# Linear attention in a decoder block: the division by the sums, with features on partitions instead of tokens

## The chip, the cores and the metric

The kernel runs on one core of a Trainium2 chip. The metric is the device time of one execution in microseconds (us). A core has five engines that run side by side and meet only at semaphores: TensorE (PE in the profile; its weight loads are PEld), VectorE (DVE), ScalarE (ACT), GpSimd (POOL) and SyncE (SP), which here only issues DMAs. Each engine works through its own instructions strictly in the order in which the program gives them, so an instruction that waits also holds up everything behind it on its engine.

## The reference

A decoder layer over 32 batches of 128 tokens with 256 features, in float32: a causal linear attention (part A), a cross attention with softmax (part B), and a gated feed-forward network, each behind a layer normalization and with a residual.

```python
def attn(x, Wq, bq, Wk, bk, Wv, bv, Wo, bo):       # 16 heads of 16 features
    q, k, v = heads(x @ Wq.T + bq), heads(x @ Wk.T + bk), heads(x @ Wv.T + bv)
    q, k = elu(q) + 1, elu(k) + 1
    kv_cum = cumsum(k[..., :, None] * v[..., None, :], axis=2)
    k_cum = cumsum(k, axis=2)
    num = einsum('bhsd,bhsde->bhse', q, kv_cum)
    den = einsum('bhsd,bhsd->bhs', q, k_cum)
    return merge(num / (den[..., None] + 1e-6)) @ Wo.T + bo

x = x + attn(layernorm(x), ...)
x = x + xattn(layernorm(x), ctx, ctx, ...)          # softmax(q k^T / 4) v, 16 heads
x = x + ffn(layernorm(x), ...)                      # w1, w2, h1, h2, w3 with row scales
```

What the change touches is the last line but one of `attn`: the division of `num` by `den` and the product with `Wo`.

## The kernel before

The work has two stages. Up to about 440 us the two attentions of all 32 batches are computed, two batches (a *pair*, index m or n) at a time; after that the feed-forward network runs over eight blocks of four batches. The residual stream x of all batches stays in SBUF (`xs`).

**Part A, linear attention, for one pair.** `a_norm` takes the statistics on DVE (`pair_stats`; the inverse root by Newton steps on POOL) and normalizes on POOL. `a_transpose` puts features on partitions. `a_keys` and `a_queries` project (`project`) and apply `phi`: two ScalarE passes and one DVE pass; the queries are then masked on POOL by head parity (`masked`, factors in `col`). `a_values` projects with tokens on partitions into `va`, where each head has 32 columns: 16 values, then 16 ones. For each batch j of the pair:

- `a_scores(m, j)`: products of keys and queries into four PSUM banks (`scores_banks`, tag s0 and s1, one buffer of each), in the profile *sa*. DVE multiplies by the causal mask into `at` (L494).
- `a_weighted(m, j)` calls `weighted`: 16 small products (*pf*, L404) with `at` as the moving operand. The result has features on partitions: in each group g of 32 partitions 16 rows of a head's numerator and 16 rows that all hold its denominator (from the ones). ScalarE copies it to SBUF as `fa` (L412).
- `a_divide(m, j)` calls `divided`: four PE transposes (*po*, L419) put tokens on partitions; DVE adds epsilon (L423), inverts the 16 denominators of each token (L424) and multiplies (L428) into `oa`.
- `a_turn(m, j)`: two transposes (*pot*, L512) put features on partitions again; ScalarE copies to `oT` (L514).
- `a_out(m, j)`: the product with Wo (*pw*, L367 from L518), which DVE adds to x (L519).

**Part B, cross attention**, has the same shape with a softmax: `b_maxima` computes the scores once (*sm*) and reduces their maxima on DVE (L565); `b_turn_maxima` transposes these (*pz*) and spreads them into `mT` (L576); `b_scores` computes the scores again minus the maxima (*se*, L388 and L588) and ScalarE takes the exponent (L598); `b_weighted` and `b_divide` are as in part A, with `fb` and `ob`. *sm*, *sa* and *se* share the same four PSUM banks, so each has to wait until the one before has been read. All other PSUM tiles come from four buffers (`bank`).

**What sets the order.** `manual_schedule` makes the order in the program the order of PE, ACT, DVE and POOL. It is written out by hand as lists of units, each (function, pairs ahead, batch). The list `both` is one step of the steady state (L613): part A works on pair m, part B on pair m-3, and each step has two halves, one for each batch. `first` (L621) is for the first three steps, `begins` (L646), `alone` and `last` for those in which the feed-forward network already starts. A unit that has been done is skipped. SP's DMAs are not in such a list; they are issued in an order that the compiler chooses, each when its buffers are free. On SP's queue there are the loads of x, weights and context (`cT`, b_load), the second loads of weights, which DVE compares with the first (`again`, `test`), and the stores of the output.

```python
both = [
    (b_maxima, 0, 0), (b_weighted, -1, 1), (a_divide, -1, 1), (b_transpose, 1), (b_values, 1),
    (a_scores, 0, 0), (b_turn_maxima, 0, 0), (b_divide, -1, 1), (a_turn, -1, 1), (a_transpose, 1),
    (b_queries, 1), (b_scores, 0, 0), (a_weighted, 0, 0), (a_out, -1, 1), (b_norm, 2), (a_keys, 1),
    (b_maxima, 0, 1), (b_weighted, 0, 0), (a_divide, 0, 0), (a_bias, 1), (a_queries, 1),
    (a_scores, 0, 1), (b_turn_maxima, 0, 1), (b_divide, 0, 0), (a_turn, 0, 0), (b_keys, 1),
    (b_scores, 0, 1), (a_weighted, 0, 1), (a_out, 0, 0), (a_norm, 2), (a_values, 1), (b_load, 2),
]
```

The functions that the change touches, and what calls them:

Of the kernel before, what the change touches and what calls it, by code (L numbers as in the profile page):

```python
# [32 lines left out]
A_TAGS = {"xna", "xTa", "e", "r", "ka", "qa2", "at0", "at1", "fa", "oa", "oT"}  # L33
# [13 lines left out]
def decoder_block_kernel(  # L47
# [30 lines left out]
    warms = tiny.tile([P, 2], F32, name="warms")  # L78
    zero, warm = warms[:, 0:1], warms[:, 1:2]
# [182 lines left out]
    with tc.manual_schedule(engines=ORDERED):  # L262
# [133 lines left out]
        def weighted(weights, v, tag):  # L396

            pf = bank("pf")
            for i in range(4):
                for g in range(G):
                    nc.tensor.matmul(  # L404
                        pf[32 * g : 32 * g + 32, i, :],
                        lhsT=v[:, 4 * i + g, :],
                        rhs=weights[g // 2][:, g % 2, i, :],
                        start=True,
                        stop=True,
                    )  # L410
            f = buffer([P, 4, S], F32, tag=tag, name=tag)
            nc.scalar.copy(f, pf)  # L412
            return f

        def divided(f, add, tag):

            po = bank("po")
            for i in range(4):
                nc.tensor.transpose(po[:, i, :], f[:, i, :], ident)  # L419
            po = po.rearrange("p i (g w) -> p (i g) w", w=VW)  # L420
            rden = small.tile([P, H], F32, tag="rden", name="rden", bufs=2)
            if add:
                nc.vector.tensor_scalar(rden, po[:, :, HD], add, None, ALU.add)  # L423
                nc.vector.reciprocal(rden, rden)  # L424
            else:
                nc.vector.reciprocal(rden, po[:, :, HD])
# [75 lines left out]
        def a_weighted(m, j):  # L502
            A[m]["f", j] = weighted(A[m].pop(("w", j)), A[m]["v"][:, j], "fa")

        def a_divide(m, j):
            A[m]["o", j] = divided(A[m].pop(("f", j)), ATTN_EPS, "oa")

        def a_turn(m, j):
            pt = bank("pot").rearrange("p a s -> p (a s)")[:, : DC * S]
            o = A[m].pop(("o", j))  # L510
            for c in range(DC):
                nc.tensor.transpose(pt[:, ts(c, P)], o[:, ts(c, P)], ident)  # L512
            oT = buffer([P, DC, S], F32, tag="oT", name="oT")
            nc.scalar.copy(oT.rearrange("p c s -> p (c s)"), pt)  # L514
            A[m]["oT", j] = oT

        def a_out(m, j):
            pp = token_major(bank("pw").rearrange("p a s -> p (a s)")[:, :D], WO, A[m].pop(("oT", j)))  # L518
            nc.vector.tensor_tensor(xs[m][:, j, :], pp, xs[m][:, j, :], ALU.add)  # L519
# [52 lines left out]
        def b_turn_maxima(m, j):  # L572
            pz = bank("pz").rearrange("p a s -> p (a s)")[:, :S]
            nc.tensor.transpose(pz, zs[j].rearrange("p g r -> p (g r)"), ident)
            mT = buffer([P, 4, S], F32R, tag="mT", name="mT")
# [28 lines left out]
        def b_divide(m, j):  # L604
            o = divided(Bs[m].pop(("f", j)), None, "ob")
# [8 lines left out]
            (b_maxima, 0, 0), (b_weighted, -1, 1), (a_divide, -1, 1), (b_transpose, 1), (b_values, 1),  # L614
            (a_scores, 0, 0), (b_turn_maxima, 0, 0), (b_divide, -1, 1), (a_turn, -1, 1), (a_transpose, 1),
            (b_queries, 1), (b_scores, 0, 0), (a_weighted, 0, 0), (a_out, -1, 1), (b_norm, 2), (a_keys, 1),
            (b_maxima, 0, 1), (b_weighted, 0, 0), (a_divide, 0, 0), (a_bias, 1), (a_queries, 1),
            (a_scores, 0, 1), (b_turn_maxima, 0, 1), (b_divide, 0, 0), (a_turn, 0, 0), (b_keys, 1),
            (b_scores, 0, 1), (a_weighted, 0, 1), (a_out, 0, 0), (a_norm, 2), (a_values, 1), (b_load, 2),
        ]  # L620
        first = [  # L621
            (a_scores, 0, 0), (a_norm, 2), (a_turn, -1, 1), (a_keys, 1), (a_out, -1, 1), (b_norm, 2),
            (a_weighted, 0, 0), (a_bias, 0), (a_scores, 0, 1), (a_divide, 0, 0), (a_queries, 1),
            (b_transpose, 1), (a_values, 1), (a_weighted, 0, 1), (a_turn, 0, 0), (a_bias, 1),
            (b_queries, 1), (a_transpose, 2), (a_out, 0, 0), (a_divide, 0, 1), (b_load, 2),
# [12 lines left out]
        def settle():  # L638
# [303 lines left out]
```

## Time and profile before

| | us |
|---|---|
| median of the runs | 1135.98 (1135.59 to 1137.45, 3 runs) |
| the profiled execution, as timed | 1138.04 |
| span of its profile | 1136.2 |
| granted TensorE clock, mean | 0.997 of full speed |
| L428 DVE product oa<-po,rden, 128x256 | 0.425 each, 32 times |
| L412 ACT copy fa<-pf, 128x512 | 0.592 each, 32 times |
| L514 ACT copy oT<-pot, 128x256 | 0.373 each, 32 times |
| L519 DVE x<-pw,x, 128x256 | 0.425 each, 32 times |
| L565 DVE reduction nm<-sm, 128x1024 | 1.217 each, 64 times |

A line of the groups reads: line of the kernel, engine, operation, output<-inputs, shapes and count, then busy time in all and the mean of one in ns, then the idle time of that engine just before these instructions and what ended it. A line of the order in time reads: start, length, engine, line, operation, names, shapes and count, and in brackets the idle time before it with its releaser. Matmuls are pipelined: a group of four transposes of 0.27 us each takes 0.66 us, and the next group starts before that time is over, so what a group costs is read from the distance between the starts of successive groups. A line of busy time by stretches gives the stretch and its length, then busy time and count of PE, PEld, DVE, ACT and POOL, then the granted TensorE clock, the share of the DMA engines and GB/s.

### The profile page before, as it was taken

The numbers are of one execution on the slowest core, as the hardware profiler recorded it, in microseconds if no ns is written. First come the engines' busy times: TensorE is split into PE (matmuls) and PEld (weight loads), VectorE is DVE, ScalarE is ACT, GpSimd is POOL, SyncE is SP. The second block draws the span as 40 slices with busy tenths as digits, with TensorE's granted clock in tenths as the row PEclk, the third lists the DMA queues.
The fourth block names the chain that finished last, engine by engine and source line by source line (L and its number), as shares of the span: only waits on it lengthen the run. The fifth ranks groups of instructions, "written<-read, shape, count | busy, mean of one in ns | idle before, by whom it ended". The sixth has DMA issues, their size and how long they took to land.

```text
span 1136.2 us, 20345 instructions
## 1 busy us (share of the span) xinstructions
PE 1117.1 (98%) x8238; PEld 902.7 (79%) x8238; DVE 577.3 (51%) x1296; ACT 411.4 (36%) x655; POOL 446.8 (39%) x1025
## 2 busy tenths in 40 slices
PE   8899999999999999999999999999999999999997
PEld 6677777777777777767888888888888888888886
DVE  6667777777777776532243433522522522422411
ACT  4344444444444446861221221321311312312311
POOL 3655555555555546454231321321311312312311
PEclk9999999999999999999999999999999999999999
DMA  8001111111111100005000111000000000000000
GB/s 274 1 20 48 47 48 48 48 48 48 48 48 48 48 11 11 1 1 185 20 26 31 38 38 38 19 14 5 29 5 5 19 1 2 18 1 15 5 1 22
DMA packets 26548, 39.28 MB, mean 35 GB/s; under 512 B 2512, under 2 KB 18640, under 8 KB 26448
## 3 DMA queue, kind: packets, MB, share of 16 engines
q1 hardware_dynamic: 22000, 26.09, 6.8%
q0 software_dynamic: 4032, 11.54, 3.2%
q8 instruction: 67, 1.10, 0.4%
q10 hardware_dynamic: 416, 0.28, 0.1%
q14 instruction: 33, 0.27, 0.1%
HBM read 33.71 MB, written 4.19 MB: 33 GB/s over the span
## 4 chain that ended last, share of the span: by engine, by line
PE 88%; DVE 3%; POOL 3%; ACT 2%; issue 2%; DMA 1%; SPq 0%; POOLq 0%; DVEq 0%; ACTq 0%
PE ph L218 47%; PE pp L359 9%; PE py L762 5%; PE pf L404 5%; PE pv L367 4%; PE se L388 3%; PE sa L388 3%; PE sm L388 3%; PE pw L367 3%; PE po L419 2%; PE pt L349 1%; DMA H<-in_h2T_dram 1%; DVE at L494 1%; PE se L588 1%; DVE nm L565 1%
## 5 line engine op out<-in xcount | busy, mean ns | idle before, releaser
L181 DVE TENSOR_TENSOR gl<-hg,gh 128x512 fp32r<-128x512 f32 x126 | 87.7, 696 | 345.5 <-POOL gh L180 342.6
L180 POOL CAST gh<-hg 128x512 fp32r<-128x512 f32 x128 | 79.1, 618 | 362.0 <-ACT hg L242 362.0
L242 ACT ACTIVATE hg<-ph,col 128x512 f32<-128x512 f32 x128 | 88.3, 690 | 366.8 <-PE ph L218 366.8
L218 PE MATMUL ph<-sl,H 128*128 128x512 f32 x512 | 199.3, 389 | 0.8 <-POOL sl L181 0.8
L218 PE MATMUL ph<-gl,H 128*128 128x512 f32 x512 | 199.4, 389 | 0.4 <-DVE gl L181 0.4
L218 PE MATMUL ph<-sh,H 128*128 128x512 f32 x512 | 199.6, 390 | 0.1
L218 PE MATMUL ph<-gh,H 128*128 128x512 f32 x512 | 199.4, 390 | 0.0
L218 PEld LDWEIGHTS ph<-sl,H 128*128 128x128 f32 x512 | 96.1, 188 | 21.0 <-POOL sl L181 1.2
L218 PEld LDWEIGHTS ph<-gl,H 128*128 128x128 f32 x512 | 96.1, 188 | 21.0 <-DVE gl L181 1.1
L218 PEld LDWEIGHTS ph<-sh,H 128*128 128x128 f32 x512 | 96.1, 188 | 20.9 <-POOL sh L180 0.6
L218 PEld LDWEIGHTS ph<-gh,H 128*128 128x128 f32 x512 | 96.1, 188 | 20.4 <-POOL gh L180 0.6
L218 PE MATMUL ph<-xh,W 128*128 128x512 f32 x256 | 100.6, 393 | 0.0
L218 PE MATMUL ph<-xl,W 128*128 128x512 f32 x256 | 99.8, 390 | 0.0
L180 POOL CAST sh<-hs 128x512 fp32r<-128x512 f32 x64 | 58.5, 915 | 66.8 <-DVE hs L234 66.8
L565 DVE TENSOR_REDUCE nm<-sm 128x8 f32<-128x1024 f32 x64 | 75.2, 1217 | 17.6 <-PE sm L388 17.6
L494 DVE TENSOR_TENSOR at<-sa,causal 128x1024 f32<-128x1024 f32 x64 | 75.2, 1215 | 8.0 <-PE sa L388 8.0
L232 ACT ACTIVATE sil<-ph,col 128x512 f32<-128x512 f32 x64 | 44.1, 689 | 74.9 <-PE ph L218 74.8
L234 DVE SCALAR_TENSOR_TENSOR hs<-ph,col,sil 128x512 f32<-128x512 f32 x64 | 48.0, 750 | 36.2 <-PE ph L218 20.1
L598 ACT ACTIVATE pr<-se 128x1024 f32<-128x1024 f32 x64 | 62.0, 1022 | 11.9 <-PE se L588 11.9
L146 POOL TENSOR_TENSOR t<-rstd 128x2 f32<-128x2 f32 x138 | 32.5, 235 | 83.3 <-DVE hv L143 76.1
L359 PE MATMUL pp<-xTa,WA 128*128 128x256 f32 x256 | 62.2, 388 | 0.7 <-ACT xTa L351 0.7
L762 PE MATMUL py<-W,gh 128*128 128x256 f32 x256 | 62.6, 285 | 0.0
(133 smaller groups left out, 1933.3 us busy)
## 6 DMA issues: line engine op xcount, KB each, us to landing
x<-in_x_dram SPq DMA_DIRECT2D x16, 256.0 KB, 5.7
cT<-in_ctxT_dram SPq DMA_DIRECT2D x16, 256.0 KB, 2.6
stage<-in_h1T_dram SPq DMA_DIRECT2D x16, 256.0 KB, 2.8
H<-in_h1T_dram POOLq DMA_DIRECT2D x8, 512.0 KB, 3.6
H<-in_h2T_dram POOLq DMA_DIRECT2D x8, 512.0 KB, 8.1
out_dram<-y SPq DMA_DIRECT2D x32, 128.0 KB, 1.7
raw<-in_h2T_dram SPq DMA_DIRECT2D x16, 256.0 KB, 2.8
WA<-in_wattn_dram SPq DMA_DIRECT2D x4, 256.0 KB, 4.7
```

Of the source, the lines that this page charges most:

```text
L180: (high_engine.copy if high_engine is nc.scalar else high_engine.tensor_copy)(high, t)
L181: lows.append(lambda: low_engine.tensor_tensor(low, t, high.bitcast(F32), ALU.subtract))
L218: nc.tensor.matmul(pp, lhsT=w[:, k, ts(c, P)], rhs=parts[p], start=(k == 0 and p == 0), stop=(k == len(src) - 1 and p == 1),)
L242: nc.scalar.activation(t, pp, AF.Gelu, scale=col[:, c_scale + c : c_scale + c + 1])
L359: nc.tensor.matmul(pp[:, c, :], lhsT=w[:, d, ts(c, P)], rhs=src[:, d, :], start=(d == 0), stop=(d == DC - 1))
L367: nc.tensor.matmul(pp, lhsT=src[:, d, :], rhs=w[:, d, :], start=(d == 0), stop=(d == DC - 1))
L388: nc.tensor.matmul(sc[g // 2][:, g % 2, 2 * c : 2 * c + 2, :], lhsT=loaded[32 * g : 32 * g + 32, c, ts(j, S)], rhs=streamed[32 * g : 32 * ...
L404: nc.tensor.matmul(pf[32 * g : 32 * g + 32, i, :], lhsT=v[:, 4 * i + g, :], rhs=weights[g // 2][:, g % 2, i, :], start=True, stop=True,)
L494: nc.vector.tensor_tensor(at.rearrange("p g i s -> p (g i) s"), sc[u].rearrange("p g i s -> p (g i) s"), causal.unsqueeze(1).to_broadcast( ...
L565: nc.vector.tensor_reduce(nm[:, 2 * u : 2 * u + 2, :], sc[u], AX.X, ALU.max, negate=True)
L598: nc.scalar.activation(pr, sc[u], AF.Exp)
L762: nc.tensor.matmul(py[:, :D], lhsT=h[k][p][:, ts(j, S)], rhs=W3[:, k, :], start=(k == 0 and p == 0), stop=(k == HC - 1 and p == 1),)
```

## The change

Part A no longer goes to tokens on partitions and back. `weighted` takes a bias: for part A the copy from PSUM adds epsilon to the denominator rows (`eps`, a column that holds 1e-6 on those rows and 0 on the others). From `fa`, 16 DMAs from SBUF to SBUF on SP's queue (for each of two targets, four groups and two head parities one, 16 partitions by 2 by 128 elements each) bring the 16 numerator rows of each head to `vc` and its 16 denominator rows to `dc`, the same partitions in both. `a_divide` inverts `dc` in place (128x256) and multiplies `vc` by it into `oa`, which already has features on partitions; `a_turn` is gone, and `a_out` takes `oa`. The columns of Wo are put into the matching order on the host, as those of Wq and Wk are already. The order lists are changed, `mT` has one buffer instead of two, and 20 instead of 12 idle transposes run at the start. Part B still divides as before.

```diff
-        def weighted(weights, v, tag):
+        def weighted(weights, v, tag, add=None):
...
             f = buffer([P, 4, S], F32, tag=tag, name=tag)
-            nc.scalar.copy(f, pf)
+            if add is None:
+                nc.scalar.copy(f, pf)
+            else:
+                nc.scalar.activation(f, pf, AF.Identity, bias=add)
             return f
...
         def a_weighted(m, j):
-            A[m]["f", j] = weighted(A[m].pop(("w", j)), A[m]["v"][:, j], "fa")
+            f = weighted(A[m].pop(("w", j)), A[m]["v"][:, j], "fa", eps)
+            f = f.rearrange("p (c e) s -> p e c s", e=2)
+            vc, dc = (buffer([P, DC, S], F32, tag=tag, name=tag) for tag in ("vc", "dc"))
+            for n, t in enumerate((dc, vc)):
+                for g in range(G):
+                    for e in range(2):
+                        from_row = 32 * g + HD * (1 - n)
+                        to_row = 32 * g + HD * e
+                        nc.sync.dma_start(out=t[to_row : to_row + HD], in_=f[from_row : from_row + HD, e])
+            A[m]["o", j] = vc, dc
 
         def a_divide(m, j):
-            A[m]["o", j] = divided(A[m].pop(("f", j)), ATTN_EPS, "oa")
-
-        def a_turn(m, j):
-            pt = bank("pot").rearrange("p a s -> p (a s)")[:, : DC * S]
-            o = A[m].pop(("o", j))
-            for c in range(DC):
-                nc.tensor.transpose(pt[:, ts(c, P)], o[:, ts(c, P)], ident)
-            oT = buffer([P, DC, S], F32, tag="oT", name="oT")
-            nc.scalar.copy(oT.rearrange("p c s -> p (c s)"), pt)
-            A[m]["oT", j] = oT
+            vc, dc = A[m]["o", j]
+            nc.vector.reciprocal(dc, dc)
+            A[m]["o", j] = o = buffer([P, DC, S], F32, tag="oa", name="oa")
+            nc.vector.tensor_tensor(o, vc, dc, ALU.mult)
...
-            mT = buffer([P, 4, S], F32R, tag="mT", name="mT")
+            mT = buffer([P, 4, S], F32R, tag="mT", name="mT", bufs=1)
...
         both = [
-            (b_maxima, 0, 0), (b_weighted, -1, 1), (a_divide, -1, 1), (b_transpose, 1), (b_values, 1),
-            (a_scores, 0, 0), (b_turn_maxima, 0, 0), (b_divide, -1, 1), (a_turn, -1, 1), (a_transpose, 1),
-            (b_queries, 1), (b_scores, 0, 0), (a_weighted, 0, 0), (a_out, -1, 1), (b_norm, 2), (a_keys, 1),
-            (b_maxima, 0, 1), (b_weighted, 0, 0), (a_divide, 0, 0), (a_bias, 1), (a_queries, 1),
-            (a_scores, 0, 1), (b_turn_maxima, 0, 1), (b_divide, 0, 0), (a_turn, 0, 0), (b_keys, 1),
-            (b_scores, 0, 1), (a_weighted, 0, 1), (a_out, 0, 0), (a_norm, 2), (a_values, 1), (b_load, 2),
+            (b_maxima, 0, 0), (b_weighted, -1, 1), (a_divide, -1, 0), (a_out, -1, 0), (b_values, 1),
+            (a_scores, 0, 0), (b_turn_maxima, 0, 0), (b_divide, -1, 1), (b_transpose, 1), (a_transpose, 1),
+            (b_queries, 1), (b_scores, 0, 0), (a_weighted, 0, 0), (a_keys, 1),
+            (b_maxima, 0, 1), (b_weighted, 0, 0), (a_divide, -1, 1), (a_bias, 1), (a_queries, 1),
+            (a_scores, 0, 1), (b_turn_maxima, 0, 1), (b_divide, 0, 0), (a_out, -1, 1), (b_norm, 2), (b_keys, 1),
+            (b_scores, 0, 1), (a_weighted, 0, 1), (a_divide, 0, 0), (a_out, 0, 0), (a_norm, 2), (a_values, 1),
+            (b_load, 2),
         ]
         first = [
-            (a_scores, 0, 0), (a_norm, 2), (a_turn, -1, 1), (a_keys, 1), (a_out, -1, 1), (b_norm, 2),
-            (a_weighted, 0, 0), (a_bias, 0), (a_scores, 0, 1), (a_divide, 0, 0), (a_queries, 1),
-            (b_transpose, 1), (a_values, 1), (a_weighted, 0, 1), (a_turn, 0, 0), (a_bias, 1),
-            (b_queries, 1), (a_transpose, 2), (a_out, 0, 0), (a_divide, 0, 1), (b_load, 2),
+            (a_scores, 0, 0), (a_norm, 2), (a_keys, 1), (a_divide, -1, 0), (a_out, -1, 0),
+            (a_weighted, 0, 0), (a_bias, 0), (a_scores, 0, 1), (a_queries, 1), (a_divide, -1, 1),
+            (b_transpose, 1), (a_values, 1), (a_weighted, 0, 1), (a_bias, 1), (a_out, -1, 1), (b_norm, 2),
+            (b_queries, 1), (a_transpose, 2), (b_load, 2),
         ]
...
         begins = [
-            (b_load, 2), (b_maxima, 0, 0), (b_weighted, -1, 1), (a_divide, -1, 1), (b_transpose, 1),
-            (b_values, 1), (b_turn_maxima, 0, 0), (a_turn, -1, 1), (b_divide, -1, 1), (a_out, -1, 1), beside,
-            (b_queries, 1), (b_scores, 0, 0), beside,
-            (b_norm, 2), (b_maxima, 0, 1), settle, (b_weighted, 0, 0), beside,
-            (b_turn_maxima, 0, 1), (b_divide, 0, 0), settle, (b_keys, 1), (b_scores, 0, 1), beside,
+            (b_load, 2), (b_maxima, 0, 0), (b_weighted, -1, 1), (b_transpose, 1), (b_values, 1),
+            (b_turn_maxima, 0, 0), (b_divide, -1, 1), (b_queries, 1), (b_scores, 0, 0), (b_keys, 1),
+            (a_divide, -1, 1), (a_out, -1, 1), beside,
+            (b_maxima, 0, 1), (b_norm, 2), (b_weighted, 0, 0), beside,
+            (b_turn_maxima, 0, 1), (b_divide, 0, 0), settle, (b_scores, 0, 1), beside,
         ]
...
-        for n in range(12):
+        for n in range(20):
             nc.tensor.transpose(idle[:, n % 4, :], ident, ident)
         a_norm(0)
+
+        nc.vector.tensor_scalar(eps, col[:, C_PAR + 1 : C_PAR + 2], ATTN_EPS, None, ALU.mult)
```

More of the change, by code (lines that the diff above doesn't have):

```diff
@@ L32 @@
 ATTN_EPS = 1e-6
-A_TAGS = {"xna", "xTa", "e", "r", "ka", "qa2", "at0", "at1", "fa", "oa", "oT"}
+A_TAGS = {"xna", "xTa", "e", "r", "ka", "qa2", "at0", "at1", "fa", "vc", "dc", "oa"}
 ORDERED = {getattr(mybir.EngineType, n) for n in ("PE", "Activation", "DVE", "Pool")}
@@ L76, in decoder_block_kernel @@
     make_upper_triangular(nc, causal, val=1.0, diag=True)
-    warms = tiny.tile([P, 2], F32, name="warms")
-    zero, warm = warms[:, 0:1], warms[:, 1:2]
+    warms = tiny.tile([P, 3], F32, name="warms")
+    zero, warm, eps = (warms[:, n : n + 1] for n in range(3))
     nc.vector.memset(zero, 0.0)
@@ L411, in weighted, with divided @@
             f = buffer([P, 4, S], F32, tag=tag, name=tag)
-            nc.scalar.copy(f, pf)
+            if add is None:
+                nc.scalar.copy(f, pf)
+            else:
+                nc.scalar.activation(f, pf, AF.Identity, bias=add)
             return f
-        def divided(f, add, tag):
+        def divided(f, tag):
             po = bank("po")
@@ L421, in divided @@
             rden = small.tile([P, H], F32, tag="rden", name="rden", bufs=2)
[L422 to L426, printed above, removed]
+            nc.vector.reciprocal(rden, po[:, :, HD])
             o = buffer([P, D], F32, tag=tag, name=tag)
@@ L502, in a_weighted @@
         def a_weighted(m, j):
-            A[m]["f", j] = weighted(A[m].pop(("w", j)), A[m]["v"][:, j], "fa")
-        def a_divide(m, j):
-            A[m]["o", j] = divided(A[m].pop(("f", j)), ATTN_EPS, "oa")
-        def a_turn(m, j):
-            pt = bank("pot").rearrange("p a s -> p (a s)")[:, : DC * S]
-            o = A[m].pop(("o", j))
-            for c in range(DC):
-                nc.tensor.transpose(pt[:, ts(c, P)], o[:, ts(c, P)], ident)
-            oT = buffer([P, DC, S], F32, tag="oT", name="oT")
-            nc.scalar.copy(oT.rearrange("p c s -> p (c s)"), pt)
-            A[m]["oT", j] = oT
+            f = weighted(A[m].pop(("w", j)), A[m]["v"][:, j], "fa", eps)
[8 more added lines that the diff above has]
+            A[m]["o", j] = vc, dc
+        def a_divide(m, j):
+            vc, dc = A[m]["o", j]
+            nc.vector.reciprocal(dc, dc)
+            A[m]["o", j] = o = buffer([P, DC, S], F32, tag="oa", name="oa")
+            nc.vector.tensor_tensor(o, vc, dc, ALU.mult)
         def a_out(m, j):
-            pp = token_major(bank("pw").rearrange("p a s -> p (a s)")[:, :D], WO, A[m].pop(("oT", j)))
+            pp = token_major(bank("pw").rearrange("p a s -> p (a s)")[:, :D], WO, A[m].pop(("o", j)))
             nc.vector.tensor_tensor(xs[m][:, j, :], pp, xs[m][:, j, :], ALU.add)
@@ L604, in b_divide @@
         def b_divide(m, j):
-            o = divided(Bs[m].pop(("f", j)), None, "ob")
+            o = divided(Bs[m].pop(("f", j)), "ob")
             nc.gpsimd.tensor_tensor(xs[m][:, j, :], xs[m][:, j, :], o, ALU.add)
@@ L903 @@
             [
-                (a[n][by_group] if n[-2:] in ("Wq", "Wk") else a[n]).T
+                (a[n][by_group] if n[-2:] in ("Wq", "Wk") else a[n][:, by_group] if n[-2:] == "Wo" else a[n]).T
                 for n in (
```

## The prediction

> **What bounds the kernel now.** I read the busy shares first, then the shares of the chain that ended last.
>
> ```profile
> PE 1117.1 (98%) x8238; PEld 902.7 (79%) x8238; DVE 577.3 (51%) x1296; ACT 411.4 (36%) x655; POOL 446.8 (39%) x1025
> PE 88%; DVE 3%; POOL 3%; ACT 2%; issue 2%; DMA 1%; SPq 0%; POOLq 0%; DVEq 0%; ACTq 0%
> ```
>
> TensorE (PE) seems to be everything. But the change lies in the attention stage, before 440 us, so I looked at that stretch alone, in the view of busy time by stretches.
>
> ```profile
> 200.00:300.00 100.00, 99.92 (x1114) 76.23 (x1113) 78.44 (x199) 48.18 (x85) 60.10 (x168) 1.00 0.15 49
> ```
>
> PE is full there, but VectorE (DVE, the third pair) is at 78%: what leaves PE and lands on DVE is not free. Then the groups of the removed work:
>
> ```profile
> L419 PE MATMUL po<-ident,fa 128*128 128x128 f32 x128 | 20.8, 285 | 0.0
> L512 PE MATMUL pot<-ident,oa 128*128 128x128 f32 x64 | 12.5, 277 | 0.0
> L423 DVE TENSOR_SCALAR rden<-po 128x16 f32<-128x16 f32 x32 | 5.3, 167 | 0.0
> L424 DVE RECIPROCAL rden<-rden 128x16 f32<-128x16 f32 x32 | 8.1, 253 | 1.1
> ```
>
> Then one steady step in order of time. A step treats one pair of batches; sm (b_maxima) of its first half starts at 207.69 and of the next step at 236.31, so it lasts 28.62 us: first half 14.40, second half 14.22. This is the second half (columns: start, us, what):
>
> ```profile
> 222.09 1.15 PE L388 MATMUL sm<-kb,qb 32*128 32x256 f32 x16
> 223.84 0.69 DVE L467 SCALAR_TENSOR_TENSOR ka<-e,r 128x512 f32<-128x512 f32 x1 [1.33 <-ACT r L465]
> 226.49 1.50 PE L388 MATMUL sa<-qa,ka 32*128 32x256 f32 x16
> 227.13 0.17 DVE L423 TENSOR_SCALAR rden<-po 128x16 f32<-128x16 f32 x1
> 228.09 0.60 PE L419 MATMUL po<-ident,fb 128*128 128x128 f32 x4
> 228.52 0.38 PE L512 MATMUL pot<-ident,oa 128*128 128x128 f32 x2
> 228.82 2.34 DVE L494 TENSOR_TENSOR at<-sa,causal 128x1024 f32<-128x1024 f32 x2
> 231.08 0.68 DVE L576 TENSOR_TENSOR mT<-pz,sel 128x512 fp32r<-128x512 f32 x1
> 232.51 1.08 PE L404 MATMUL pf<-at,va 128*32 128x128 f32 x32
> 233.52 1.13 PE L367 MATMUL pw<-WA,oT 128*128 128x256 f32 x4
> 234.69 0.42 DVE L519 TENSOR_TENSOR x<-pw,x 128x256 f32<-128x256 f32 x1 [2.31 <-PE pw L367]
> ```
>
> The reader is to see that in this half PE runs just behind DVE. sa takes 1.50 us instead of 1.15, because its PSUM banks come free only when DVE's reduction of sm ends (226.80); the exponent product se waits for mT. DVE's only slack is its 2.31 us before x.
>
> **The change, part by part.** *Removed from PE.* Starts of successive groups give what each costs in the stream: the four po transposes of fa 0.49 us (252.79 to 253.28), the two pot 0.22 (228.52 to 228.74). That is 0.71 per batch, 22.7 for 32 batches, the most the change can bring where PE is the bound. From ScalarE goes oT (0.37), which delays nobody; fa's copy becomes an activation with a bias, between the 0.59 of the copy and the 0.69 of the scaled 128x512 activation (L549), hidden in its idle time.
>
> *Moved.* In the old steady step a_divide stood behind each b_weighted and one a_out in each half. In the new order of the instructions both a_divide and both a_out stand in the second half, and with them b_norm's statistics. DVE then runs there: reduction, **a_divide(-1,1)**, phi, mask, mT, b_divide, x of a_out(-1,1), b_norm, **a_divide(0,0)**, x of a_out(0,0), a_norm, va. PE runs sm, pf, queries, sa, pz, po, **pw(-1,1)**, keys, se, pf, **pw(0,0)**, pv, next sm. So pw(0,0) waits for a division that is queued behind everything DVE does in the half, and pv and sm are queued behind pw.
>
> *Added on DVE.* The reciprocal is now over 128x256. No row shows it. Lower bound: its surplus over an ordinary operation is fixed and elements cost (683-425)/256 = 1.0 ns (rows of 128x512 and 128x256), so 0.253+240*1.0 = 0.50 us. Upper bound: the surplus is per element; ordinary 128x16 operations take 0.167 to 0.199, so it is 3.4 to 5.4 ns, and 0.425+256*that = 1.29 to 1.80. I take **1.6**, as the 16-element row is the same operation, and what it takes beyond its neighbours looks like work per element. The product stays at 0.42 (same shape). [...]
>
> *The second half with 1.6 us, on the clock of the trace above.* The reciprocal starts at 227.13 as rden did and ends at 228.73; the product is done at 229.2. po now ends at 228.52 as before (sa was held by DVE, so the po removed ahead of it brings nothing). pw(-1,1) thus waits 0.7 and starts at 229.23; with 0.97 for pw and 1.82 for keys, se starts at 232.02, its first part takes 0.78, the rest 0.70: pf from 233.50 to 234.51. DVE: product+0.37, phi 0.62, mask 2.26 put mT at 232.01; 1.22 later x, 1.97 for the statistics (249.08 to 251.05): the second reciprocal starts at 235.20, the product is done at 237.27. pw(0,0) starts at 237.32, a **PE stall of 2.8 us** where there was none. pv at 238.29, next sm at 240.11 instead of 236.31: **+3.8**.
>
> *First half.* pw starts 4.95 before DVE's reduction (233.52 to 238.47) as before, so DVE is again late by the same 2.16 after sm. sa ends at +5.63 instead of +5.91. Then pz 0.17, po 0.44, both pt 0.86, a wait of 0.43 for xTb (transposed only 1.3 us earlier now), queries 1.92, se 1.31, pf 1.01, keys 1.82: 13.6 instead of 14.4, **-0.8**. Step: +3.0.
>
> *Transfers.* Each batch adds 16 DMAs of 16 KB on SP's queue. Issues there:
>
> ```profile
> 0.73 0.44 SPq L280 DMA_DIRECT2D x<-in_x_dram  x1
> 1.24 0.46 SPq L290 DMA_DIRECT2D cT<-in_ctxT_dram  x1
> 7.56 9.48 SPq L280 DMA_DIRECT2D x<-in_x_dram  x12
> ```
>
> One every 0.51 us, 0.79 when a run of large ones backs up. Landing is bounded by the smallest in the page, 1.7 to 2.0 us (out_dram, raw of w3). fa(0,0) ends about 0.26 before sm, 221.8; 16*0.51+2.0 later, at 232.0, all has landed, 3.2 us before the second reciprocal wants it: hidden. At 0.79 it would be 236.4, 1.2 late. The batch with j=1 has half a step more. 32 issues, cT and two test loads take 18 of a step's 31.6 us on SP; they wait for fa, then cT, needed a step later, waits for them. Other small edits (eps, eight more idle transposes while the first loads are under way, mT with one buffer, whose reader is 14 us past) cost nothing that shows; without the loads as cover the transposes are 8*0.11 = 0.9.
>
> *First steps.* Step 1: mask 31.5 to 33.8, statistics 1.7, ka 0.7, reciprocal and product 2.1: pw(0,0) at 38.3, with PE idle since the keys (33.3); pf at 39.3 instead of 36.3. Step 2's scores wait for POOL at 48.85 anyhow, so 0.6 is left; step 2 loses likewise, and the first sm comes some 3.6 late. Last step (16): two transposes groups fewer, -0.7.
>
> *Clock.* One row bears on stalls: PE busy 1.35 of 3.40 us, next stretch at half clock.
>
> ```profile
> 46.80:50.20 3.40, 1.35 (x19) 1.00 (x19) 0.38 (x2) 0.00 (x0) 3.36 (x6) 1.00 0.00 0
> 50.20:53.70 3.50, 3.50 (x11) 2.78 (x10) 3.40 (x8) 0.37 (x1) 0.00 (x0) 0.51 0.00 0
> ```
>
> The idle before it was 2.79 us, like the new stall; the product after it took 3.54 instead of 1.89, so 1.65 lost. Between nothing and 1.65 in each of 13 steps is 0 to 21; I take half the steps at 1.4, +9. [...] The row shows the clock falling after 2.79 us.
>
> *Sum.* 13 steps (66 to 437 us) * 3.0 = 39, +3.6, -0.7, +9 = +51 on the profiled span of 1136.2; the median of the runs shown, 1135.98, is 0.2 below that: **1187 us**.
>
> **Rivals.** *Cheap reciprocal* (0.50): oa(-1,1) no longer delays PE, but pw(0,0) still waits 1.5 (235.2 against 233.7): second half +1.7, step +0.9, no clock loss worth counting: 11+1-0.7, 1147. For: nothing shows the slope; against: the 16-element row. *Late transfers*: 0.79 per issue, 1.2 more per step, 1203. For: the run of twelve; against: those are 256 KB each. *PE gets its gift*: the division of a_divide(0,0) is ready when pf ends, and the 22.7 come through: 1113. Place: pw(0,0); it decides if DVE's chain from sm is 2.8 us shorter than laid out; a cheap reciprocal gives 1.3 of that relative to pf, and the rest would have to come from b_norm or the mask, whose rows don't vary. *Evens out*: the same chain short by half, 1136.
>
> **How the numbers follow.** Forecast 0.55, late transfers 0.12, cheap reciprocal 0.17, gift 0.13, even 0.03. 0.2% (2.3 us) is about what runs can tell. Faster 0.13, same 0.03, slower 0.84. With 1.80 for the reciprocal (+5) and the whole clock loss (+12) the forecast reaches 1204, late transfers beyond; the low end goes below the cheap reciprocal: 1142 to 1212.
>
> **What would show it.** pw idle before it, put down to DVE oa, some 2.8 and 0.7 us a step; reciprocal 1.6; step 31.6; DVE near 85%; half-clock stretches after stalls; PE transposes L419 halved. Wrong if the new pw waits for nothing, if its releaser is a DMA, or if the reciprocal is near 0.5.

## The result, and the profile after

| | before | after |
|---|---|---|
| median of the runs, us | 1135.86 (1135.59 to 1137.45) | 1225.70 (1224.59 to 1226.62) |
| span of the profiled execution, us | 1136.2 | 1224.5 |
| granted TensorE clock, mean | 0.997 | 0.974 |
| one steady step, us | 28.6 | 34.1 |

The ratio is 1.0787, with an interval of [1.0769, 1.0806]: slower, as forecast, but by 90 us where 51 were forecast, and outside the range.

First the page of after: busy shares, the shares of the chain that ended last, the group of the output products, and the transfers of the sums. The second fence has the same group in before.

```profile
PE 1127.2 (92%) x8054; PEld 901.2 (74%) x8054; DVE 623.6 (51%) x1265; ACT 400.8 (33%) x623; POOL 444.5 (36%) x1025
...
PE 70%; DVE 13%; SPq 8%; ACT 3%; issue 3%; DMA 3%; POOL 1%; DVEq 0%; ACTq 0%; POOLq 0%
...
L367 PE MATMUL pw<-WA,oa 128*128 128x256 f32 x128 | 45.2, 487 | 75.0 <-DVE oa L519 70.1
...
dc<-fa SPq DMA_DIRECT2D x256, 16.0 KB, 1.8
```

```profile
L367 PE MATMUL pw<-WA,oT 128*128 128x256 f32 x128 | 36.0, 403 | 0.5 <-ACT oT L514 0.5
```

PE has 184 instructions fewer and is still busy 10 us longer: a part of its work ran at half clock (pw takes 487 ns instead of 403 each). 75.0 us of idle PE stand ahead of pw, where it was 0.5, nearly all put down to the DVE product oa. In the chain SP's queue has appeared with 8%, about 98 us; that figure is kept in mind for the second experiment.

The view of busy time by stretches shows the attention stage and three neighbouring stretches of one step (columns as before: PE, PEld, DVE, ACT, POOL, clock, DMA share, GB/s).

```profile
245.40:248.80 3.40, 0.41 (x2) 0.41 (x3) 2.65 (x6) 1.63 (x3) 2.14 (x10) 1.00 0.02 5
248.80:252.30 3.50, 3.50 (x10) 2.77 (x9) 1.91 (x9) 0.00 (x0) 1.70 (x6) 0.51 0.11 28
252.30:255.70 3.40, 3.40 (x55) 2.42 (x54) 2.75 (x6) 0.58 (x1) 2.65 (x10) 1.00 0.10 25
200.00:300.00 100.00, 85.85 (x881) 63.96 (x874) 76.02 (x165) 38.00 (x65) 48.61 (x143) 0.95 0.19 56
```

PE is busy 0.41 of 3.40 us, and in the next 3.5 us it runs at half clock; then the clock is back. In the last line PE is no longer full: 85.85 of 100 us where it was 99.92. Nor is DVE: 76.02. Nobody is the bound for long; the engines wait for each other in turn.

The second half of the same step in order of time, as it was shown for before:

```profile
232.22 1.15 PE L388 MATMUL sm<-kb,qb 32*128 32x256 f32 x16
237.65 1.75 DVE L517 RECIPROCAL dc<-dc 128x256 f32<-128x256 f32 x1 [0.20 <-DMA dc<-fa]
239.44 0.42 DVE L519 TENSOR_TENSOR oa<-vc,dc 128x256 f32<-128x256 f32 x1
240.01 1.10 PE L367 MATMUL pw<-WA,oa 128*128 128x256 f32 x4 [1.08 <-DVE oa L519]
242.65 0.68 DVE L580 TENSOR_TENSOR mT<-pz,sel 128x512 fp32r<-128x512 f32 x1
246.04 1.75 DVE L517 RECIPROCAL dc<-dc 128x256 f32<-128x256 f32 x1
247.82 0.42 DVE L519 TENSOR_TENSOR oa<-vc,dc 128x256 f32<-128x256 f32 x1
248.39 1.65 PE L367 MATMUL pw<-WA,oa 128*128 128x256 f32 x4 [3.24 <-DVE oa L519]
249.83 3.08 PE L367 MATMUL pv<-WA,xTa 128*128 128x256 f32 x8
252.84 1.15 PE L388 MATMUL sm<-kb,qb 32*128 32x256 f32 x16
```

The half lasts 20.62 us (232.22 to 252.84) instead of 14.22, the other half 13.45 instead of 14.40. Both waits of pw are where the prediction put them: 1.08 and 3.24 us behind the product. What it did not put into every step is the half clock: from pw to the next sm 4.45 us pass instead of 2.79, since pw and pv run at half speed, 1.66 us more.

**Where the 88.3 us between the two spans are**, by the starts of sm in both traces:

| stretch | before | after | difference | forecast |
|---|---|---|---|---|
| steps 0 to 2, until the first sm | 66.40 | 76.60 | +10.2 | +3.6 |
| step 3, the first with both attentions | 26.8 | 39.8 | +12.9 | +3.7 |
| steps 4 to 14, eleven steps | 28.6 each | 34.1 each | +60.5 | +40.7 |
| step 15 | | | +4.8 | +3.7 |
| step 16 and the feed-forward network | | | -0.1 | -0.7 |

(The forecast of 3.7 per step is 3.0 and its part of the 9 us for the clock.)

### The profile page after: what moved, and what is told of

The parts are those of the page before. It is cut to its first block, busy times and chain, and to the rows that moved or that the text cites. A ratio compares the mean times of both kernels' runs of the same rounds, so it can differ in the third digit from the quotient of the medians.

```text
span 1224.5 us, 20845 instructions
## 1 busy us (share of the span) xinstructions
PE 1127.2 (92%) x8054; PEld 901.2 (74%) x8054; DVE 623.6 (51%) x1265; ACT 400.8 (33%) x623; POOL 444.5 (36%) x1025
## 4 chain that ended last, share of the span: by engine, by line
PE 70%; DVE 13%; SPq 8%; ACT 3%; issue 3%; DMA 3%; POOL 1%; DVEq 0%; ACTq 0%; POOLq 0%
PE ph L218 46%; SPq L512 8%; PE pv L367 5%; PE py L769 4%; PE pp L359 4%; DVE dc L517 3%; DVE at L493 3%; PE pw L367 2%; PE pf L404 2%; PE sm L388 2%; PE sa L388 1%; DVE nm L569 1%; PE se L388 1%; DVE oa L519 1%; DMA cT<-in_ctxT_dram 1%
## 5 line engine op out<-in xcount | busy, mean ns | idle before, releaser
L367 PE MATMUL pw<-WA,oa 128*128 128x256 f32 x128 | 45.2, 487 | 75.0 <-DVE oa L519 70.1
L367 PEld LDWEIGHTS pw<-WA,oa 128*128 128x128 f32 x128 | 25.5, 219 | 85.5 <-issue 69.2
L569 DVE TENSOR_REDUCE nm<-sm 128x8 f32<-128x1024 f32 x64 | 75.2, 1215 | 17.1 <-PE sm L388 17.1
L180 POOL CAST sh<-hs 128x512 fp32r<-128x512 f32 x64 | 58.6, 915 | 61.6 <-DVE hs L234 61.6
```

Of the source, the lines that this page charges most:

```text
L180: (high_engine.copy if high_engine is nc.scalar else high_engine.tensor_copy)(high, t)
L367: nc.tensor.matmul(pp, lhsT=src[:, d, :], rhs=w[:, d, :], start=(d == 0), stop=(d == DC - 1))
L569: nc.vector.tensor_reduce(nm[:, 2 * u : 2 * u + 2, :], sc[u], AX.X, ALU.max, negate=True)
```

## The experiments

Twelve more kernels ran. Steps are measured from sm to sm of one batch position in the steady stretch; the ratio is to the kernel before on the same chip.

| kernel | us | ratio | step, us | clock |
|---|---|---|---|---|
| after | 1225.7 | 1.0787 [1.0769, 1.0806] | 34.1 | 0.974 |
| old_order | 1318.8 | 1.1607 [1.158, 1.1634] | 41.2 | 0.924 |
| no_transfers | 1216.3 | 1.0693 [1.0658, 1.0728] | 31.9 to 34.3 | 0.975 |
| busy_wait | 1211.2 | 1.0649 [1.061, 1.0687] | 32.5 | 0.985 |
| busy_all | 1207.3 | 1.0626 [1.0601, 1.065] | 32.5 | 0.996 |
| next_half_busy | 1189.1 | 1.0469 [1.0451, 1.0486] | 31.1 | 0.995 |
| next_half | 1188.1 | 1.0442 [1.0414, 1.047] | 31.1 | 0.992 |
| next_half_busy2 | 1183.3 | 1.0422 [1.0405, 1.0439] | 31.1 | 0.994 |
| cheap_recip | 1181.8 | 1.039 [1.0357, 1.0423] | 30.4 | 0.988 |
| before_inplace | 1157.4 | 1.0177 [1.0153, 1.0201] | 29.9 | 0.995 |
| next_half_cheap | 1154.0 | 1.0161 [1.0144, 1.0178] | 29.3 | 0.992 |
| idle20 (before) | 1133.8 | 0.9984 [0.9973, 0.9996] | 28.6 | 0.999 |
| before_inplace_cheap | 1123.2 | 0.9876 [0.9853, 0.9899] | 27.5 | 0.994 |

### What the reciprocal costs: cheap_recip

```diff
-            nc.vector.reciprocal(dc, dc)
+            nc.vector.tensor_scalar(dc, dc, 1.0, None, ALU.mult)
```

> The 128x256 reciprocal is replaced by a multiplication by 1.0 of the same tile (so nothing is divided). Theory (the division stands on DVE in front of pw(0,0), and the PE stall there also halves the TensorE clock for 3.4 us in every step): DVE's chain is 2.7 us shorter, the stall before pw(0,0) falls from 3.2 us to under 2, the clock stays up in most steps, the step falls from 34.1 us to about 29.8, the kernel to 1160 to 1175 us. Rival (the 16 transfers and SP's queue set the step): less than 15 us of gain, 1210 or more.

Measured 1181.8, 44 us less, half of the loss over before. The group of the reciprocals in after, and the output products of a step of this kernel in order of time:

```profile
L517 DVE RECIPROCAL dc<-dc 128x256 f32<-128x256 f32 x32 | 56.1, 1752 | 5.1 <-DMA dc<-fa 2.6 <-issue 0.6
```

```profile
222.38 1.03 PE L367 MATMUL pw<-WA,oa 128*128 128x256 f32 x4
229.31 1.10 PE L367 MATMUL pw<-WA,oa 128*128 128x256 f32 x4 [1.85 <-DVE oa L519]
...
260.39 0.42 DVE L519 TENSOR_TENSOR oa<-vc,dc 128x256 f32<-128x256 f32 x1 [1.44 <-DMA cT<-in_ctxT_dram]
260.96 1.10 PE L367 MATMUL pw<-WA,oa 128*128 128x256 f32 x4 [3.16 <-DVE oa L519]
```

The reciprocal takes 1.752 us, the multiply 0.29. With it the first pw of the half waits for nothing, the second still 1.85 us: this rest is not the reciprocal's, it is the place of the division behind everything that DVE does in the half. The step is 30.4 us and mostly without half clock (granted 1.00 from 200 to 300 us). The last two lines are from a step in which DVE's product had itself waited 1.44 us for a transfer (the profile names the load of the context, issued right behind this batch's numerators on the same queue). Once DVE's chain is shorter, the transfers come into view. That is a part of why the time stayed above the expectation; the ordinary step, 30.4 us where 29.8 were expected, is another.

### What the transfers cost: no_transfers

```diff
-            f = f.rearrange("p (c e) s -> p e c s", e=2)
-            vc, dc = (buffer([P, DC, S], F32, tag=tag, name=tag) for tag in ("vc", "dc"))
-            for n, t in enumerate((dc, vc)):
...
+            vc, dc = f[:, 0:DC], f[:, DC : 2 * DC]
```

> The 16 DMAs of each batch are left out; the division and the product read two halves of fa as they lie (wrong values, same shapes). Theory: transfers are hidden; what goes is only DVE's handling of the DMA semaphores (0.2 to 0.5 us a division) and some of the first three steps, and the step may even stay locked at 34.1 us: 1210 to 1226 us. Rival (transfers set the time): back to within 25 us of the kernel before, 1136 to 1160.

Measured 1216.3: taking out the 512 DMAs brings 9 us. That disposes of the 8% of the chain. The chain follows, at each step, whoever came last, and a release that came 0.2 us after the next candidate takes the whole stretch behind it; what goes away with a link is the distance to that next candidate, not the link's share. The output products of two successive steps:

```profile
214.99 1.10 PE L367 MATMUL pw<-WA,oa 128*128 128x256 f32 x4 [3.01 <-DVE oa L512]
...
247.75 2.05 PE L367 MATMUL pw<-WA,oa 128*128 128x256 f32 x4 [3.00 <-DVE oa L512]
```

The stall is nearly the same, 3.0 us. In the first step the clock stays, in the second pw runs at half speed (2.05 instead of 1.10). The half-clock stretches of this trace start at 182.58 and 247.44, among others, 19 times 3.41 us apart. On this grid the first stall is cut in two: PE is busy 2.08 us from 209.9 to 213.3 and 1.71 us from 213.3 to 216.7. The second falls mostly into one stretch: PE is busy 0.74 us from 244.0 to 247.4, and then the half clock begins. So a stall of about 3 us is at the edge here: whether it costs the clock depends on where it falls.

Eight of the eleven steady steps lost the clock; ahead of each loss the stretch of the grid held 0.40 to 1.31 us of busy PE. In the other three steps, which take 32.0 us, none held less than 1.5. The 9 us are a sum of opposites: the first sm comes at 80.81 instead of 76.60, with more half clock before it, while step 3 is 2.0 us shorter and the eleven steady steps 10.0.

### What the clock costs: busy_wait and busy_all

```diff
         def a_out(m, j):
+            if j == 0 and m >= prologue:
+                warmer = bank("warmer")
+                for n in range(26):
+                    nc.tensor.transpose(warmer[:, n % 4, :], ident, ident)
             pp = token_major(...)
```

> 26 idle transposes of the identity are put on PE ahead of pw(0,0) from step 3 on; they fit into the 3.2 us in which PE waits. Theory (the stall costs a second time through the clock): no half clock after these stalls, pw and pv take 2.8 instead of 4.5 us, the step falls from 34.1 to about 32.4, the kernel by some 20 us to 1200 to 1210. Rival (the clock falls but DVE sets the step, so it costs nothing): 1222 to 1228, step 34.1 with the clock at 1.0.

Measured 1211.2. The stall is as long as before, but PE spends it on transposes that nobody reads:

```profile
212.40 3.06 PE L525 MATMUL warmer<-ident 128*128 128x128 f32 x26
215.62 1.13 PE L367 MATMUL pw<-WA,oa 128*128 128x256 f32 x4 [0.16 <-DVE oa L519]
216.59 1.89 PE L367 MATMUL pv<-WA,xTa 128*128 128x256 f32 x8
218.41 1.15 PE L388 MATMUL sm<-kb,qb 32*128 32x256 f32 x16
```

pw takes 1.13 instead of 1.65, pv 1.89 instead of 3.08, the step 32.5 instead of 34.1. The eleven steps together take 16 us less, the clock's share of them (one of them still lost it). The total fell by less, because here the first sm came at 82.15 instead of 76.60: the stretches at half clock happened to fall elsewhere in the first steps. What is left of the steady step without the clock, 32.5 against 28.6, is the plain wait, +3.9 us; the prediction had it at +3.0.

The same ahead of every output product, 44 and 16 transposes in the first steps and 26 and 8 later:

```diff
         def a_out(m, j):
+            busy = (44, 16)[j] if m < prologue else (26, 8)[j]
+            warmer = bank("warmer")
+            for n in range(busy):
+                nc.tensor.transpose(warmer[:, n % 4, :], ident, ident)
```

> As e4_busy_wait, with idle transposes ahead of every pw: 44 and 16 in the first steps (batch 0, batch 1), 26 and 8 later. Theory: the clock stays at full speed in the first four steps too; there 17 us of half clock cost up to 8 us, so 8 to 14 us less than e4_busy_wait, 1197 to 1204 us, and the step stays at 32.5. Rival (the first steps are slow because of the waits alone, not of the clock): 1208 to 1213.

Measured 1207.3, between the theory and its rival. The first sm came at 74.09 instead of 76.60, the step is the same 32.5; but step 4 still started at 114.90, 1.5 us ahead of after's 116.36. So in step 3 a part of the gain was given back, to the edit itself. This is PE in that step:

```profile
103.45 3.47 PE L359 MATMUL pp<-cT,WB 128*128 128x256 f32 x8 [2.20 <-DVE mT L584]
...
109.32 3.06 PE L525 MATMUL warmer<-ident 128*128 128x128 f32 x26
```

The keys of part B, which in after follow pw without a gap, wait 2.20 us until DVE has read pz into mT: the transposes have taken one of the four PSUM buffers, and the next free one is that of pz. Then the keys run at half clock (3.47 us). And the 26 transposes delay a pw whose oa had been ready at 108.33.

### Where the division stands: next_half, old_order

```diff
         both = [
-            (b_maxima, 0, 0), (b_weighted, -1, 1), (a_divide, -1, 0), (a_out, -1, 0), (b_values, 1),
+            (b_maxima, 0, 0), (b_weighted, -1, 1), (b_values, 1),
...
-            (b_queries, 1), (b_scores, 0, 0), (a_weighted, 0, 0), (a_keys, 1),
+            (a_divide, -1, 0), (b_queries, 1), (b_scores, 0, 0), (a_weighted, 0, 0), (a_out, -1, 0), (a_keys, 1),
...
-            (b_scores, 0, 1), (a_weighted, 0, 1), (a_divide, 0, 0), (a_out, 0, 0), (a_norm, 2), (a_values, 1),
+            (b_scores, 0, 1), (a_weighted, 0, 1), (a_norm, 2), (a_values, 1),
```

> Only the order is changed: division and output product of batch 0 move from the end of their step to the first half of the next one, behind b_divide and a_weighted there. Theory: pw no longer waits for a division queued behind b_norm; the second half falls from 20.6 to about 14.7 us, the first grows from 13.4 to about 15.1, step 29.8, no half clock in the steady steps, the kernel at 1170 to 1180 us. Rival (DVE's extra load or the transfers as such, not where they are queued): step above 32.5, 1205 or more.

Measured 1188.1: 38 us come back by order alone, with every instruction kept. The step is 31.1 us and without half clock (granted 1.00 from 200 to 300 us); step 3 takes 28.2 us instead of 39.8, since the output of the third pair's first batch no longer heads it. PE's waits in a steady step:

```profile
209.81 0.98 PE L349 MATMUL pt<-ident,xna 128*128 128x128 f32 x4 [1.26 <-POOL xna L339]
215.26 1.13 PE L367 MATMUL pw<-WA,oa 128*128 128x256 f32 x4 [0.42 <-DVE oa L519]
225.73 1.10 PE L367 MATMUL pw<-WA,oa 128*128 128x256 f32 x4 [1.09 <-DVE oa L519]
```

The long wait has gone, and three short ones are left. That of 1.26 us for POOL is new, and it is what the expectation of 29.8 missed: the normalization of part A (xna) stands on POOL behind that of part B. In after POOL begins this work 6.9 us ahead of the next sm, under the stall (245.91 to 252.84); here it begins 1.1 us ahead (200.53 to 201.63) and is busy with it until 210.3.

The opposite: the steady list of before, less the turns, with the transfers kept. (With this list the division and output of the first batch of the third pair never come: one of the 32 batches goes without its linear attention.)

> The changed kernel with the steady order of before (each a_divide right behind b_weighted of the half in which it stood, one a_out in each half, b_norm in the first half), only a_turn left out. Theory: the transfers of a batch take 10.7 us of issues on SP and land about 12.4 us after fa; in the old places DVE asks for them about 7 us too early in each half, waits with everything behind it, and the step grows to 42 to 46 us, the kernel to 1300 to 1340 us; the waits are put down to DMA. Rival (the new order is what costs, transfers are quick): step near 31, 1165 to 1180 us.

Measured 1318.8, a hit. The waits of this kernel, line that waits, what it waited for, us in total, times and the longest:

```profile
DVE oa L519 <- DMA vc<-fa: 78.6, 25, 3.9
```

In the old places DVE waits up to 3.9 us for the numerators, in most halves, and PE's exponent products behind it wait for DVE's mask (3.81 and 3.51 us in one step). The clock is in this step too: in nearly every half it falls for 6.83 us (granted 0.84 in the mean from 200 to 300 us). These stretches come 20.48 us apart, six times 3.41, and a half takes 20.5 us on average. So the new order is no accident: fa leaves ScalarE some 12 us before its 16 transfers have landed, and only a division put off that long does not wait for them.

### Reciprocal and order together: next_half_cheap

```diff
 # next_half, and
-            nc.vector.reciprocal(dc, dc)
+            nc.vector.tensor_scalar(dc, dc, 1.0, None, ALU.mult)
```

> The kernel of next_half (division and output of the first batch moved into the next half step) with the reciprocal replaced by a multiply by 1.0 of the same size, so nothing is divided. Theory: in next_half the step of 31.11 us still holds waits of pw on oa of 0.42 and 1.09 us, and both are the reciprocal's (1.75 us each, 0.29 us for the multiply); they go, the 1.26 us wait of pt on POOL stays or shrinks: a step of 29.6 to 29.9, no half clock in the steady steps, and the first steps shortened by about as much as the cheap reciprocal alone shortened them (2.7 us): 1188 - 12 x 1.35 - 3 = 1169, 1163 to 1175. Rival: with the reciprocal gone the transfers end last there, a step of 30.5 or more with DVE waiting on a DMA ahead of the multiply: 1178 or more.

Measured 1154.0, below the theory's band: the step went to 29.3, and the first steps gained more than thought (step 4 starts at 98.95 instead of 107.87). The stretch of 200 to 300 us:

```profile
200.00:300.00 100.00, 95.67 (x1027) 70.72 (x1031) 74.09 (x177) 45.58 (x82) 54.89 (x159) 1.00 0.21 62
```

PE is nearly full again, and of the waits only that for POOL is left (1.25 us).

### The first steps: next_half_busy and next_half_busy2

```diff
 # next_half, and
         def a_out(m, j):
+            busy = (44, 16)[j] if m < prologue else 0
+            warmer = bank("warmer") if busy else None
+            for n in range(busy):
+                nc.tensor.transpose(warmer[:, n % 4, :], ident, ident)
```

> The kernel of next_half with 44 and 16 idle transposes ahead of the two output projections of the first three steps alone, as in busy_all. Theory: the half clock of the first steps costs time that is not given back: the first sm comes at 74 instead of 79.65 us and the later steps stay at 31.11, so 1188 - 5.5 = 1182.5, 1180 to 1185. Rival: what is gained there is lost in the first steps with both attentions, or a shifted phase against the windows of the clock brings half clock into the steady steps: 1187 or more.

Measured 1189.1, the rival's number, but by a fault of the edit: m counts pairs, not steps, and the third pair's outputs fall into step 3. There 5.0 us of transposes ran ahead of a pw that had not waited in next_half, and the keys waited 2.21 us for a PSUM buffer, as in busy_all; the first sm had come at 73.74 instead of 79.65, step 4 at 110.90 instead of 107.87. The edit mended (`m < prologue - 1`):

> The kernel of next_half_busy with the idle transposes ahead of the output projections of the first two pairs alone: there, those of the third pair fell into the first step with both attentions, where they took 5.0 us ahead of a pw that had not waited. Theory: the half clock of the first three steps costs 5.9 us that is not given back: first sm at 73.7 us, the step after it as in next_half (28.2 us to the start of step 4, at 102 instead of 107.9), later steps 31.1: 1182, 1180 to 1185. Rival: something else (a load of weights, a shifted phase against the windows of the clock) takes the place of what is gained: 1187 or more.

Measured 1183.3, near the theory. The output products of the first three steps, in after and then here:

```profile
38.99 2.04 PE L367 MATMUL pw<-WA,oa 128*128 128x256 f32 x4 [4.90 <-issue]
51.50 1.10 PE L367 MATMUL pw<-WA,oa 128*128 128x256 f32 x4 [2.30 <-DVE oa L519]
61.54 2.08 PE L367 MATMUL pw<-WA,oa 128*128 128x256 f32 x4 [5.50 <-DVE oa L519]
73.10 1.10 PE L367 MATMUL pw<-WA,oa 128*128 128x256 f32 x4 [1.86 <-DVE oa L519]
```

```profile
40.18 1.06 PE L367 MATMUL pw<-WA,oa 128*128 128x256 f32 x4
50.30 1.10 PE L367 MATMUL pw<-WA,oa 128*128 128x256 f32 x4 [0.41 <-DVE oa L519]
60.34 1.13 PE L367 MATMUL pw<-WA,oa 128*128 128x256 f32 x4 [0.70 <-DVE oa L519]
70.53 1.10 PE L367 MATMUL pw<-WA,oa 128*128 128x256 f32 x4
```

Stalls of 4.9 and 5.5 us each brought half clock behind them (2.04 and 2.08 us). In next_half they are 4.61 and 5.53 us, with pw at 2.05 and 2.07. With PE kept busy step 4 comes at 102.25 instead of next_half's 107.87: 5.6 us, of which 4.8 reach the end; one steady step fell to half clock (33.1 us instead of 31.1).

The first three steps are the same in after, next_half and busy_wait, and yet the first sm comes at 76.60, 79.65 and 82.15 us: behind the first 25 us their traces have 10.2, 17.1 and 23.9 us of half clock. Here it is 3.4 us and the first sm at 74.03. So in after the clock costs some 2.6 us of the first steps, and what stays of their +10.2 is 7.6.

### The parts alone, in the old order: before_inplace and before_inplace_cheap

The kernel before, its order untouched, without transposes, transfers and epsilon; the division reads the halves of fa in place, so the values are not the right ones. In before_inplace_cheap a multiply by 1.0 stands for the reciprocal.

```diff
-            A[m]["f", j] = weighted(A[m].pop(("w", j)), A[m]["v"][:, j], "fa")
+            f = weighted(A[m].pop(("w", j)), A[m]["v"][:, j], "fa")
+            A[m]["o", j] = f[:, 0:DC], f[:, DC : 2 * DC]
...
-            A[m]["o", j] = divided(A[m].pop(("f", j)), ATTN_EPS, "oa")
+            vc, dc = A[m]["o", j]
+            nc.vector.reciprocal(dc, dc)
+            A[m]["o", j] = o = buffer([P, DC, S], F32, tag="oa", name="oa")
+            nc.vector.tensor_tensor(o, vc, dc, ALU.mult)
```

> The kernel before with its own order, without the transposes and without any transfer: the halves of fa are read in place, the second inverted over 128x256 and multiplied into the first (so the values divided are not the right ones, and epsilon is left out). Theory: the order that the transfers need and the reciprocal's length are what costs; in the old order the reciprocal (1.75 against 0.42 us for the two small operations it replaces) stands ahead of mask and mT, so each half gains up to 0.7 us on PE and loses up to 1.3 on DVE: 1140 to 1160, no clock loss in the steady steps. Rival: the reciprocal alone explains most of the loss wherever it stands: 1180 or more.

> The same with a multiply by 1.0 in place of the reciprocal, so nothing is inverted: what the removal of the transposes is worth by itself when the division costs DVE no more than before. If PE alone bounds the step, 0.71 us per batch come through, 1113; if PE runs behind DVE in both halves, as the second half of the step before showed, only what is not covered by DVE comes through: 1118 to 1130. Theory: the latter.

Measured 1157.4 and 1123.2, both in the theory's bands; but two of the eleven steady steps of the first lost the clock (31.56 us instead of 29.92), which the theory had excluded. The stretch of 200 to 300 us of the one and of the other:

```profile
200.00:300.00 100.00, 93.85 (x1011) 69.27 (x1007) 84.48 (x178) 44.25 (x79) 60.92 (x169) 1.00 0.13 44
```

```profile
200.00:300.00 100.00, 99.67 (x1125) 75.67 (x1121) 81.51 (x204) 47.40 (x81) 59.87 (x173) 1.00 0.16 54
```

With the multiply PE stays full and the step is 27.5 us, 1.15 less than before: of the 1.42 us of transposes in a step most comes through. With the reciprocal PE waits for DVE and the step is 29.9. This gives the sum of the change, each part by a pair of runs that differ in little else:

| part | from, to | us |
|---|---|---|
| transposes removed | before 1135.9, before_inplace_cheap 1123.2 | -12.7 |
| multiply to reciprocal | 1123.2, before_inplace 1157.4 | +34.2 |
| old order to new | 1157.4, no_transfers 1216.3 | +58.9 |
| transfers | 1216.3, after 1225.7 | +9.4 |

The small edits (bias, eps, mT's buffers, idle transposes) are in the third line too. The clock is in it as well: some 13 us, eight steady steps at 1.65. Only the second pair ran side by side on one chip; by the ratios to before on the same chip the four parts are -14.1, 34.2, 58.6 and 10.7. Nor do the parts simply add up: the reciprocal is worth 34 us here and in next_half (1188.1 to 1154.0), but 44 in the order of after.

### The idle transposes at the start: idle20

The change also puts 20 idle transposes at the start in place of 12. Alone in the kernel before:

> The kernel before with 20 instead of 12 idle transposes at the start, the only part of the change that showed a gain in its trace (the first product of scores at 17.63 instead of 18.78 us). Theory: they keep the clock up until the first context has landed; 1.0 to 1.3 us less than before, 1134.7. Rival (a difference of that one execution): no change.

Measured 1133.8 (12 runs), ratio 0.9984 [0.9973, 0.9996]. The start of before, and of this kernel:

```profile
1.47 2.82 PE L700 MATMUL idle<-ident 128*128 128x128 f32 x12 [1.47 <-POOL ident masks.py:199]
5.67 3.75 PE L359 MATMUL pp<-cT,WB 128*128 128x256 f32 x8 [1.38 <-DMA cT<-in_ctxT_dram]
```

```profile
1.46 4.35 PE L700 MATMUL idle<-ident 128*128 128x128 f32 x20 [1.46 <-POOL ident masks.py:199]
6.00 1.97 PE L359 MATMUL pp<-cT,WB 128*128 128x256 f32 x8 [0.19 <-DMA cT<-in_ctxT_dram]
```

Twelve end 1.38 us before the first context lands; eight products then take 3.75 us. Twenty reach it, and the eight take 1.97; sa follows at 17.55 instead of 18.78 us. The gain is 0.16%; its interval leaves out zero, though barely, and it is the one part of the change that helps by itself.

## Why the prediction was right in its sign and wrong in its size

The span grew by 88 us where 51 were forecast. Of the 37 that are missing, by the table of stretches, some 10 are the clock of the steady steps, 10 their plain wait (0.9 us a step too small), 9 step 3, 7 the first steps, and the rest the end.

- **Which wait, and where: right.** pw(0,0) waits for a division that is queued behind b_norm. Forecast 2.8 and 0.7 us for the two output products, measured 3.24 and 1.08. next_half shows that the place makes it: the same instructions in another order, and the wait is 0.42 and 1.09.
- **The reciprocal: nearly right.** Taken as 1.6, measured 1.752, inside the two bounds. The upper bound, from the 16-element row, came nearer than the lower one of 0.50. Twice 0.15 us, and on the first of the two divisions 0.20 us ahead of it that the profile puts down to the transfers, are part of why the plain wait was +3.9 instead of +3.0 a step.
- **The transfers: nearly right in the sum, wrong as to what they are.** Priced at nothing, they are nearly hidden: a steady step at full clock takes 32.5 us with them (busy_wait) and 32.0 without, and taking them out brings 9 us in all. But each issue takes about 0.63 us on SP (eight in 5.05), between the 0.51 and 0.79 of the bounds, and the order that hides their 12 us costs 59 with what follows from it. The prediction priced order and transfers as separate terms; old_order shows that one is the price of the other.
- **The first half: right.** Forecast -0.8, measured -0.95.
- **The clock: this step failed.** "I take half the steps at 1.4, +9." The trace has one stretch at half clock in every steady step, and 1.66 us lost by each, 18 us over eleven steps; with PE kept busy in the stall, 16 (busy_wait) and 17 (busy_all) of them come back. For these steps 7.6 had been forecast. The row of the kernel before was right; halving it was not. This steady loop did not draw at random where its stall fell. The stretches at half clock are 3.41 us long and come 34.13 us apart (at 214.68 and 248.81 us, for two), ten times their length and only 0.06 more than the step; so the stall met nearly the same point each time. That a loss stretches the step until it fits is what one would think, but no run varied the step finely enough to show it. no_transfers, with steps that do not fit (32.0 us without the loss), lost the clock in eight of eleven. Nor was PE wholly idle ahead of a loss: in after 0.41 us of work in 3.40 did not keep the clock up.
- **The first steps: this term was mis-sized.** "The first sm come some 3.6 late" was 10.2. Of these 7.6 stay when PE is kept busy (next_half_busy2) and are plain waiting in the main: the sum had one stall in each of steps 1 and 2, and the trace has two (4.90 and 2.30, 5.50 and 1.86 us). Nor did POOL's wait at 48.85 take up the first: step 2's scores start at 52.97. The other 2.6 are the half clock behind the two long stalls, which the prediction did not charge to them, and which was longer in other runs.
- **Step 3: not laid out at all.** It was counted as one more step at 3.0 and its part of the clock. It cost 12.9, because the output of the third pair's first batch, left over from the step before, heads it on PE, and pw(2,0) waits 5.27 us there and runs at half clock (2.07 us). In next_half, where it no longer heads the step, step 3 takes 28.2 us.

```profile
83.02 2.07 PE L367 MATMUL pw<-WA,oa 128*128 128x256 f32 x4 [5.27 <-DVE oa L519]
```

- **The rivals.** The cheap reciprocal's 1147 did not happen and, even with a multiply of 0.29 us, comes out at 1182: that rival charged nothing for the clock and the first steps. Late transfers is refuted by no_transfers. The gift of 22.7 us was the most the change could bring; the runs put the transposes at 12.7, with no transfers, no reciprocal and the old order.
- **What would show it.** Idle time ahead of pw, its releaser and the reciprocal's row came as named. The step did not (34.1 for 31.6), nor DVE's share (76% for 85%, since it waits too).

What stays open: how much of the 9 us of the transfers is DVE's waits at the semaphores (0.20 to 0.55 us ahead of a reciprocal) and how much the place of the stalls on the grid of the clock, and how the 59 us of the order divide beyond the clock and step 3.

## What to carry to other kernels

Price a removed transpose together with what it had made small: with tokens on partitions 16 sums per token were inverted in 0.25 us, with features on partitions the same sums fill 256 columns and take 1.75. A transfer that is hidden by moving its consumer costs what the new place costs, so lay out the new order's longest wait first, in the steady step and also in the first steps. And if that wait on PE nears 3 us in a loop, charge the half clock behind it to most turns (here, behind stalls of 3.24 and 3.0 us, it came in eleven and in eight of eleven), or give PE something idle to do meanwhile.

## What the runs showed of the hardware that was not expected

- A 128x256 reciprocal takes 1.752 us, a multiply by a constant of the same size 0.29, a product of two tiles 0.42. (1752-253)/240 = 6.2 ns per further element is what the two reciprocal rows give.
- The clock fell after a stretch that was not wholly idle (0.41 us busy of 3.40, a stall of 3.24) and came back after 3.41 us, or 6.83 behind some of the stalls of the first steps. In the steady steps of no_transfers a stall of some 3 us did it where it left 0.40 to 1.31 us of work in one stretch of the grid, and not where it left 1.5 or more in each.
- An idle PE in front of a wait cost more than a PE that did useless work: 26 transposes a step, read by nobody, took 1.6 us off the step.
- A batch's small DMAs from SBUF to SBUF took their time at issue: 16 KB lands in 1.8 us, but eight take 5.05 us to issue, 0.63 each.
